# A graph layer with a sorted scatter: 48 directly summed edge columns in f32 against 72 in three exact bf16 addends

## The chip, the cores and the metric

One core of one Trainium2 chip runs the kernel. The metric is the device time of one execution in microseconds (us); smaller is better. Three runs of the kernel before give 2962.37 us as their median (2954.45 to 2979.23).

## The reference

There are N = 6250 nodes with 128 features and E = 206250 edges with 128 features each. An edge adds its features to the row of its source node. Then come a linear layer over node, sum and a global row, two softplus layers, a last linear layer, a residual and a normalization over the features:

```python
edge_aggr = jnp.zeros((n, HIDDEN), dtype=x.dtype).at[row].add(edge_features)
global_expand = jnp.repeat(global_feat, reps, axis=0)
combined = jnp.concatenate([x, edge_aggr, global_expand], axis=-1) @ W_c + b_c
h = jax.nn.softplus(combined @ W1 + b1)
h = jax.nn.softplus(h @ W2 + b2)
return h @ W3 + b3          # then: _layernorm(x + this)
```

All arrays are f32 except the edge's node numbers, which are int32 and in no order that the kernel may rely on. The sum over edges is what takes the time: everything behind it lies in the last 150 us of the profile.

## The kernel before, in words

The edges lie as 128 partitions by 1612 columns; a column is 128 edges, one per partition. The nodes lie in 25 blocks of 256 (`BL`), and `sums_t` holds the sums turned, features on the partitions and nodes along the free dimension (128 x 6400 f32). A column gets into `sums_t` in one of two ways.

**Gathered columns** (1564 of them). They are cut into the 11 groups of `GROUPS`, each a number of columns and the rows per partition of a chunk (`sub`). For each group:

- `node_codes` (line 209) and `positions` (line 247) work out on VectorE and TensorE where each edge goes when the group is sorted by block of nodes. Each block is padded to whole chunks of `sub` x 128 edges, so that 1564 columns become 2262 columns of chunks.
- `load_rows` (line 635) loads ten columns in one transfer on SP's queue, three pieces ahead (`LEAD`) in five buffers; `scatter_rows` (line 652) writes each column with an indirect DMA from GpSimd (line 658) to a place in DRAM, `place`. The place was filled with -1 beforehand (`fill_rows`, line 230).
- `reduce_steps` (line 396) takes a group back while the next one is scattered: `load` reads eight columns of chunks, `match` compares the edges' codes with the 256 nodes of a block (VectorE, line 428; in the last groups ScalarE too, lines 423 and 425, in shares by `TAIL`), `product` multiplies features by matches in f32 (line 442, a 128x256 product per column), and `add` adds the sum of a chunk to its block of `sums_t` (line 459). Three buffers of `part` in PSUM lie between product and addition.

**Directly summed columns** (`DIRECT` = 48, the first ones; `direct_steps`, line 550). They are not sorted. A set of 12 columns (`SET`) is loaded in one transfer (`load`, line 571), and is compared with all nodes, in 13 windows of 512 (`WIDE`; the last has 256). A job is two columns (`QUAD`) against one window: `compare` gives 1 where the edge's node is the window's node, as max(0, 1 - |node - number|), by two activations on 128x512 and one on 128x1024 on ScalarE (lines 582 and 584); `add` multiplies the columns' features by it in f32 (line 594) and gathers the six jobs of a set and window in one PSUM tile, `direct_sum`; `total` adds that to `sums_t` (line 602). `begin` works out on VectorE the node numbers and, in `less`, their distance from each window's first node. There are 4 x 13 x 6 = 312 jobs. The step of job i does the comparison of job i, the product of job i - 2, and a total that has come due, three steps behind its last product.

**The order.** On TensorE, VectorE, ScalarE and SP the instructions stand in the order in which the program gives them. GpSimd's scatters follow in their own queue. All loads and stores of SP go in one order (`put_dma`, line 148). The main loop runs over the groups and, in each, over its pieces of ten columns: it issues a piece's load, codes and scatter, and then a share of four lists, the positions of the next group (`prep`), the reduction of the group before (`sums`), the work on the nodes' own rows in groups 3 to 5 (`other`) and the fill of the next place (`filled`), each by `AHEAD`. Direct steps are dealt out by `left` (line 702): group g from 1 to 6 gets steps in proportion to its columns less a third of the chunk columns of group g - 1 (less 9 more in groups 3 to 5). That makes 43, 63, 58, 52, 52 and 50 steps in groups 1 to 6. Below, stage g is the time from the first scatter of group g to the first of group g + 1.

The last part, behind the groups, computes the layers on 13 tiles of up to 512 nodes.

## Time and profile before

| | |
|---|---|
| three runs, median (lowest to highest) | 2962.37 us (2954.45 to 2979.23) |
| the profiled execution, its time | 2979.23 us |
| its span, first to last instruction | 2977.4 us |
| mean granted TensorE clock | 0.823 |
| busy: TensorE, VectorE, ScalarE, GpSimd | 1948.8, 1326.4, 963.2, 1587.9 us |
| first and last scatter | 25.8 and 2826.8 us |
| first scatter of groups 1 to 8 | 81.3, 264.1, 643.4, 1075.6, 1500.1, 1931.9, 2346.5, 2571.8 us |
| direct products (line 594) | 1248 records from 104.5 to 2357.2 us |
| gathered products (line 442) | 4524 records |

An f32 product stands in the trace as two records, a bf16 product as one. PE is TensorE's matmuls, PEld its weight loads, DVE VectorE, ACT ScalarE, POOL GpSimd and SP the engine whose queue issues most transfers. Matmuls are pipelined, so the distance from start to start tells their price and their shown duration does not. A row of the groups gives the busy time, the mean duration, and the idle time of the engine just before, with what ended most of it; `remote` is a release that the profile can't name. A row of the windows gives the bounds and length of a stretch, the busy time and number of instructions of each engine, the granted TensorE clock as a share of full speed, the share of the DMA engines' time and GB/s.

### The profile page before, as it was taken

What the parts mean: (1) busy time and instruction counts of PE and PEld (TensorE: products, weight loads), DVE (VectorE), ACT (ScalarE), POOL (GpSimd) and SP (SyncE); (2) the same over time, 40 slices, a digit from 0 to 9 for tenths busy, and PEclk for the clock granted to TensorE, in tenths of its full rate; (3) what the DMA queues carried; (4) which work ended last, traced back from release to release, by engine and by line L of the source; (5) the groups of instructions that cost most, each with busy time, mean ns of one, the idle gap of its engine ahead of it and who ended that gap; (6) DMA issues with size and microseconds to landing.
All of it is one profiled execution on the core that took longest, in us unless ns stands there. A gap on an engine that the chain in (4) does not pass through costs nothing.

```text
span 2977.4 us, 21943 instructions
## 1 busy us (share of the span) xinstructions
PE 1948.8 (65%) x6470; PEld 1261.6 (42%) x6470; DVE 1326.4 (45%) x1961; ACT 963.2 (32%) x1313; POOL 1587.9 (53%) x1782
## 2 busy tenths in 40 slices
PE   2244586763876845887737768628777558747876
PEld 0022243431544532554424545415545446635663
DVE  5233353522453423554314644316454356525566
ACT  0223373423432313233204223205233100024596
POOL 5766435565355554655663465563655555554405
PEclk9867797776887967988868878869988778868898
DMA  9777445653464642555543445534445445545632
GB/s 294 210 209 231 116 127 161 186 148 93 136 171 138 184 127 92 149 157 153 143 129 95 140 119 147 146 91 119 135 137 154 142 123 178 179 120 144 177 86 87
DMA packets 418894, 437.21 MB, mean 147 GB/s; under 512 B 37807, under 2 KB 308774, under 8 KB 418774
## 3 DMA queue, kind: packets, MB, share of 16 engines
q1 hardware_dynamic: 368582, 332.43, 39.8%
q0 software_dynamic: 50048, 103.35, 10.5%
q8 instruction: 52, 0.85, 0.1%
q14 instruction: 68, 0.56, 0.1%
q10 hardware_dynamic: 144, 0.02, 0.0%
HBM read 262.62 MB, written 173.03 MB: 146 GB/s over the span
## 4 chain that ended last, share of the span: by engine, by line
PE 47%; another core or an unknown queue 24%; issue 14%; DVE 7%; ACT 7%; DVEq 0%; DMA 0%; ACTq 0%
PE part L442 29%; PE direct_sum L594 14%; ACT direct_hot L582 2%; ACT direct_hot L584 2%; DVE hot L428 2%; ACT hot L423 2%; DVE sums_t L459 1%; PE small L343 1%; DVE so_far L320 1%; PE small L277 0%; PE small L339 0%; PE small L340 0%; PE small L338 0%; ACT away L787 0%
## 5 line engine op out<-in xcount | busy, mean ns | idle before, releaser
L658 POOL DMA_INDIRECT place<-rows,pos x1564 | 1505.4, 963 | 1281.0 <-DMA rows<-in_edge_attr 598.2
L442 PE MATMUL part<-hot,chunks 128*128 128x256 f32 x4524 | 1183.1, 413 | 652.7 <-issue 340.6
L442 PEld LDWEIGHTS part<-hot,chunks 128*128 128x128 f32 x4524 | 926.5, 208 | 931.9 <-issue 458.0
L582 ACT ACTIVATE direct_hot<-iota_f,less 128x512 f32<-128x512 f32 (+1 forms) x624 | 404.2, 695 | 1595.9 <-remote 838.7
L594 PE MATMUL direct_sum<-direct_hot,direct_rows 128*128 128x512 f32 (+1 forms) x1248 | 633.7, 639 | 189.1 <-ACT direct_hot L584 108.7
L459 DVE TENSOR_TENSOR sums_t<-sums_t,part 128x256 f32 x808 | 339.0, 420 | 882.0 <-remote 568.4
L428 DVE SCALAR_TENSOR_TENSOR hot<-chunks,iota_ps 128x2048 f32<-128x2048 f32 (+1 forms) x251 | 570.6, 2274 | 0.0
L594 PEld LDWEIGHTS direct_sum<-direct_hot,direct_rows 128*128 128x128 f32 x1248 | 252.6, 208 | 446.8 <-issue 302.8
L584 ACT ACTIVATE direct_hot<-direct_hot,ones 128x1024 f32<-128x1024 f32 (+1 forms) x312 | 348.0, 1115 | 10.1
L423 ACT ACTIVATE hot<-iota_f,chunks 128x256 f32<-128x256 f32 x258 | 106.5, 494 | 381.2 <-PE part L442 299.6
L352 DVE TENSOR_TENSOR at<-small,ib 128x500 f32<-128x500 f32 (+3 forms) x80 | 52.9, 662 | 105.1 <-remote 71.0
L354 DVE TENSOR_REDUCE pos<-at 128x20 int32<-128x500 f32 (+3 forms) x80 | 87.0, 1088 | 2.7
L320 DVE TENSOR_TENSOR_SCAN so_far<-iota_ps,ib 128x1500 bf16<-128x1500 f32 (+7 forms) x30 | 85.9, 2862 | 0.0
L602 DVE TENSOR_TENSOR sums_t<-sums_t,direct_sum 128x512 f32<-128x512 f32 (+1 forms) x52 | 34.5, 663 | 111.1 <-PE direct_sum L594 64.5
L533 DVE COPY x_t<-small 128x512 f32<-128x512 f32 (+1 forms) x13 | 8.6, 659 | 150.1 <-remote 115.3
L541 DVE TENSOR_SCALAR z_x<-small,z_bias 128x512 f32<-128x512 f32 (+1 forms) x13 | 9.3, 718 | 136.1 <-remote 95.6
L425 ACT ACTIVATE hot<-hot,ones 128x2048 f32<-128x2048 f32 (+2 forms) x34 | 65.1, 1914 | 1.1
L864 POOL TENSOR_TENSOR x_sb<-x_sb,b_all 128x512 f32<-128x512 f32 (+1 forms) x13 | 15.3, 1213 | 81.7 <-DMA x_sb<-in_x 81.7
L293 DVE TENSOR_REDUCE size_f<-small 128x25 f32<-128x500 f32 (+1 forms) x11 | 7.4, 674 | 115.0 <-remote 69.5
L339 PE MATMUL small<-so_far,ones_h 128*128 128x500 bf16 (+3 forms) x80 | 33.4, 417 | 21.7 <-issue 17.0
L266 DVE TENSOR_TENSOR ib<-block,iota_ps 128x1500 bf16<-128x1500 bf16 (+7 forms) x30 | 44.4, 1503 | 0.0
L277 PE MATMUL small<-ib,ones_h 128*128 128x500 bf16 (+3 forms) x80 | 24.9, 422 | 28.6 <-DVE ib L266 16.5
(117 smaller groups left out, 531.7 us busy)
## 6 DMA issues: line engine op xcount, KB each, us to landing
chunks<-place SPq DMA_DIRECT2D x281, 516.0 KB
rows<-in_edge_attr SPq DMA_DIRECT2D x154, 640.0 KB
place<-fill SPq DMA_DIRECT2D x252, 258.0 KB
place<-rows,pos POOLq DMA_INDIRECT x1564
x_sb<-in_x SPq DMA_DIRECT2D x24, 256.0 KB
direct_rows<-in_edge_attr SPq DMA_DIRECT2D x4, 768.0 KB
out<-y SPq DMA_DIRECT2D x12, 256.0 KB
src_i<-in_src SPq DMA_DIRECT2D x1, 761.5 KB
```

What stands on the lines that cost most here:

```text
L320: nc.vector.tensor_tensor_scan(t, iota_ps[:, 1:2].to_broadcast([P, NB * n]), in_block[k][0], 0.0, op0=ALU.mult, op1=ALU.add)
L352: nc.vector.tensor_mul(at, got.pop((k, j0)), in_block[k][1][:, :, j0:j1])
L354: nc.vector.tensor_reduce(pos[:, a - c0 + j0:a - c0 + j1], at.rearrange("p b g -> p g b"), axis=mybir.AxisListType.X, op=ALU.add)
L423: nc.scalar.activation(hot[:, j], codes, AF.Abs, bias=chunks[i][:, j, D:W], scale=-1.0)
L425: nc.scalar.activation(hot[:, :m], hot[:, :m], AF.Relu, bias=ones[:, :1], scale=-1.0)
L428: nc.vector.scalar_tensor_tensor(hot[:, :m], chunks[i][:, :m, D:W].to_broadcast([P, m, BL]), code_of(g), iota_ps.unsqueeze(1).to_broadcast ...
L442: nc.tensor.matmul(part[:, s - q, :], t[:, s * sub + j, :D], hot[:, s * sub + j], start=(j == 0), stop=(j == sub - 1))
L459: nc.vector.tensor_add(here, here, part[:, s - q, :])
L582: nc.scalar.activation(hot[:, j, :n], iota_f[:, :n], AF.Abs, bias=less[:, w, c + q + j:c + q + j + 1], scale=-1.0)
L584: nc.scalar.activation(hot[:, :, :n], hot[:, :, :n], AF.Relu, bias=ones[:, :1], scale=-1.0)
L594: nc.tensor.matmul(sum_of[c, w][:, :n], rows_in[c][:, q + j, :], hot[:, j, :n], start=(q + j == 0), stop=(q + j == k - 1))
L658: s = nc.gpsimd.indirect_dma_start(out=dst, out_offset=bass.IndirectOffsetOnAxis(ap=at, axis=0), in_=rows[:r, j, :], in_offset=None)
```

## The change

- `DIRECT` goes from 48 to 72 (six sets, 468 jobs); group 6 goes from 226 to 202 columns, so that the gathered columns are 24 fewer (1540, in 2238 columns of chunks). The direct steps become 476, in groups 1 to 6 by the same rule 67, 98, 90, 81, 81 and 61.
- The comparisons' result, `direct_hot`, is bf16. ScalarE's instructions are the same three per job.
- Each column's features are written as a sum of three bf16 numbers. The upper half of an f32 is read as the first where it lies; `split`, new, works on VectorE: the rest behind the first, the rest behind the upper half of that rest into `direct_low`, and a copy of the upper half of the rest into the lower half of the f32's own place. A set of 12 columns takes 18 such instructions on 128x256, in twos of columns (`SPLIT`). The f32 product of a column (two records) becomes three bf16 products with weight loads of their own.
- `less` is worked out per set (128x156) in `split`, not once for all in `begin`. `split` for the next set stands at the last window but one of a set, five windows (30 jobs) behind the set's load.
- The first set's load stands in group 0's last piece, ahead of that piece's `load_rows`; before, it was the second step of group 1, behind `begin`. The first `split` follows `begin` there.

Totals still come three steps behind the last product, and the shares of ScalarE in the last groups (`TAIL`) are the same.

```diff
...
 LOAD_COLS = 10
 EPS = 1e-5
-GROUPS = ((40, 1), (120, 2), (200, 4), (240, 4), (240, 4), (240, 4), (226, 4), (130, 2), (72, 2),
+GROUPS = ((40, 1), (120, 2), (200, 4), (240, 4), (240, 4), (240, 4), (202, 4), (130, 2), (72, 2),
           (38, 1), (18, 1))
 SOONER = 6
...
 CHUNK_ROWS = 1024
 PLACES = 3
-DIRECT = 48
+DIRECT = 72
 SET = 12
 WIDE = 512
 QUAD = 2
+SPLIT = 2
 FILL = 4
 POS_COLS = 20
 PART_COLS = 60
...
         def direct_steps():
             steps = []
             if not ND:
                 return steps
             NW = -(-NB * BL // WIDE)
-            less = keep.tile([P, NW, ND], F32, name="less")
-            rows_in, hot_of, sum_of = {}, {}, {}
+            node_f = keep.tile([P, ND], F32, name="node_f")
+            first = keep.tile([P, NW], F32, name="first")
+            less_of = {}
+            rows_in, low_in, hot_of, sum_of = {}, {}, {}, {}
             def begin():
-                first = keep.tile([P, NW], F32, name="first")
                 nc.gpsimd.iota(first, pattern=[[WIDE, NW]], base=0, channel_multiplier=0,
                                allow_small_or_imprecise_dtypes=True)
-                part, node, _ = whole_nodes(0, ND)
-                nc.vector.tensor_copy(node, part)
-                nc.vector.tensor_tensor(
-                    less, node.unsqueeze(1).to_broadcast([P, NW, ND]),
-                    first.unsqueeze(2).to_broadcast([P, NW, ND]), op=ALU.subtract)
+                part, _, _ = whole_nodes(0, ND)
+                nc.vector.tensor_copy(node_f, part)
             def load(c):
                 n = min(SET, ND - c)
...
                 sync_dma(rows_in[c][:, :n],
                          edge_attr[:P * T, :].rearrange("(p t) d -> p t d", p=P)[:, c:c + n, :])
+            def halves(t):
+                return [t.bitcast(BF16).rearrange("p c (d h) -> p c d h", h=2)[:, :, :, h]
+                        for h in (0, 1)]
+            def split(c):
+                n = min(SET, ND - c)
+                less = less_of[c] = direct_p.tile([P, NW, SET], F32, name="less", bufs=2)
+                nc.vector.tensor_tensor(
+                    less[:, :, :n], node_f[:, c:c + n].unsqueeze(1).to_broadcast([P, NW, n]),
+                    first.unsqueeze(2).to_broadcast([P, NW, n]), op=ALU.subtract)
+                low_in[c] = direct_p.tile([P, SET, D], BF16, name="direct_low", bufs=2)
+                for a in range(0, min(SET, ND - c), SPLIT):
+                    b = min(a + SPLIT, SET, ND - c)
+                    rest = direct_p.tile([P, SPLIT, D], F32, name="direct_rest")[:, :b - a]
+                    x_c = rows_in[c][:, a:b]
+                    nc.vector.tensor_sub(rest, x_c, halves(x_c)[1])
+                    nc.vector.tensor_sub(low_in[c][:, a:b], rest, halves(rest)[1])
+                    nc.vector.tensor_copy(halves(x_c)[0], halves(rest)[1])
             def compare(c, w, q):
                 n = min(WIDE, NB * BL - w * WIDE)
-                hot = direct_p.tile([P, QUAD, WIDE], F32, name="direct_hot", bufs=3)
+                hot = direct_p.tile([P, QUAD, WIDE], BF16, name="direct_hot", bufs=3)
                 hot_of[c, w, q] = hot
                 for j in range(QUAD):
                     nc.scalar.activation(hot[:, j, :n], iota_f[:, :n], AF.Abs,
-                                         bias=less[:, w, c + q + j:c + q + j + 1], scale=-1.0)
+                                         bias=less_of[c][:, w, q + j:q + j + 1], scale=-1.0)
                 nc.scalar.activation(hot[:, :, :n], hot[:, :, :n], AF.Relu, bias=ones[:, :1],
                                      scale=-1.0)
...
                 hot = hot_of.pop((c, w, q))
                 if q == 0:
                     sum_of[c, w] = ps.tile([P, WIDE], F32, name="direct_sum", bufs=2)
-                for j in range(QUAD):
-                    nc.tensor.matmul(sum_of[c, w][:, :n], rows_in[c][:, q + j, :], hot[:, j, :n],
-                                     start=(q + j == 0), stop=(q + j == k - 1))
+                for j in range(q, q + QUAD):
+                    addends = halves(rows_in[c][:, j:j + 1]) + [low_in[c][:, j:j + 1]]
+                    for i, part in enumerate(addends):
+                        nc.tensor.matmul(sum_of[c, w][:, :n], part[:, 0], hot[:, j - q, :n],
+                                         start=(j == 0 and i == 0), stop=(j == k - 1 and i == 2))
                 if q + QUAD == k:
                     ready.append((c, w, n))
...
             jobs = [(c, w, q) for c in range(0, ND, SET) for w in range(NW)
                     for q in range(0, min(SET, ND - c), QUAD)]
-            steps += [begin, lambda: load(0)]
+            steps += [lambda: load(0), begin, lambda: split(0)]
             ready, behind = [], []
             for i in range(len(jobs) + 6):
...
                         c, w, q = jobs[i]
                         if (w, q) == (NW // 2, 0) and c + SET < ND:
                             load(c + SET)
+                        if (w, q) == (NW - 2, 0) and c + SET < ND:
+                            split(c + SET)
                         compare(*jobs[i])
                     if 1 < i < len(jobs) + 2:
                         add(*jobs[i - 2])
...
             for g in range(1, G - 4):
                 left[g] = max(0.0, groups[g][1] - groups[g][0]
                               - groups[g - 1][3] * groups[g - 1][2] / 3 - (9 if 3 <= g < 6 else 0))
+            direct_first = direct[:1]
+            direct = direct[1:]
             direct_at = 0.0
             i = 0
             assert G > 6
...
                 filled = fill_rows(g + 1)
                 done = [0, 0, 0, 0]
                 for q in mine:
+                    if g == 0 and q == mine[-1]:
+                        for step in direct_first:
+                            step()
                     load_rows(i + LEAD)
                     code_rows(i)
                     scatter_rows(i)
```

## The prediction

> **What bounds the kernel now.** I read the page first, then the windows by stage (a stage runs from the first scatter of one group of columns to the first of the next), then the timeline inside single stretches. The page:
>
> ```profile
> span 2977.4 us, 21943 instructions
> PE 1948.8 (65%) x6470; PEld 1261.6 (42%) x6470; DVE 1326.4 (45%) x1961; ACT 963.2 (32%) x1313; POOL 1587.9 (53%) x1782
> PE 47%; another core or an unknown queue 24%; issue 14%; DVE 7%; ACT 7%; DVEq 0%; DMA 0%; ACTq 0%
> L658 POOL DMA_INDIRECT place<-rows,pos x1564 | 1505.4, 963 | 1281.0 <-DMA rows<-in_edge_attr 598.2
> ```
>
> No engine is full. TensorE (PE) carries 47% of the chain that ended last, and 24% belongs to waits that the profile can't name. GpSimd's scatters wait 598 us for rows, which SP sends in one queue with loads that wait for TensorE. The unnamed waits lie in the long runs of scatters:
>
> ```profile
> 1527.14 0.98 POOL L658 DMA_INDIRECT place<-rows,pos  x1 [1.60 <-issue]
> 1528.43 0.96 POOL L658 DMA_INDIRECT place<-rows,pos  x1 [0.30 <-issue]
> ...
> 1563.78 1.33 ACT L582 ACTIVATE direct_hot<-iota_f,less 128x512 f32<-128x512 f32 x2 [46.92 <-remote]
> ...
> 1572.38 2.93 PE L442 MATMUL part<-hot,chunks 128*128 128x256 f32 x6 [41.09 <-DVE hot L428]
> ```
>
> The columns are start, duration, engine and line, operation, idle time before it. A scatter of one column issues every 1.27 us; while they run without a break, TensorE, and what waits for it, stands still for 41 to 47 us. Counted over the timeline from 81 to 2571 us: in the first 15 us of a run of scatters TensorE starts 3.1 to 3.4 matmul records per us, after 30 us fewer than 0.6, and it recovers some 5 us after the run ends. Then SP's queue moves, rows land, and the next run begins. So a stage is a part that goes with the scatters, plus the time that TensorE needs in between, and there TensorE is dense:
>
> ```profile
> 1191.11 1.88 PE L594 MATMUL direct_sum<-direct_hot,direct_rows 128*128 128x512 f32 x4
> 1192.82 0.80 PE L277 MATMUL small<-ib,ones_h 128*128 128x500 bf16 x3
> 1193.47 3.61 PE L442 MATMUL part<-hot,chunks 128*128 128x256 f32 x16
> 1196.92 1.88 PE L594 MATMUL direct_sum<-direct_hot,direct_rows 128*128 128x512 f32 x4
> ```
>
> Starts give prices at full clock. A direct job (two columns against 512 nodes in f32, four records) takes 1192.82 - 1191.11 = 1.71 us; three bf16 matmuls of 500 take 0.65 us, 0.217 each, weight loads hidden; 16 gathered records take 3.45 us, 0.216 each.
>
> ```profile
> 264.10:643.40 379.30, 244.06 (x704) 135.52 (x702) 152.07 (x218) 160.83 (x207) 196.13 (x219) 0.80 0.52 150
> 1931.90:2346.50 414.60, 284.99 (x971) 186.90 (x970) 192.04 (x249) 121.12 (x153) 222.23 (x250) 0.84 0.43 127
> 2346.50:2571.80 225.30, 147.42 (x597) 118.73 (x596) 116.97 (x140) 1.63 (x3) 127.43 (x142) 0.80 0.53 158
> ```
>
> These are stages 2, 6 and 7 (time, then PE, PEld, DVE, ACT, POOL busy, granted TensorE clock, DMA). Stage 7 has 130 scatters, 568 gathered records and next to no direct work: 568 x 0.216 / 0.80 = 153 us of TensorE, so 72 us are left, **0.555 us per scattered column**. In stage 6 (227 scatters, 689 gathered records, 51 direct jobs) 126 us for the columns and 689 x 0.216 / 0.84 = 177 us leave 112 us, **2.19 us per direct job**, against 1.71 / 0.84 = 2.04 from the spacing. Stage 2 (200, 358, 68 jobs) gives 2.53 against 2.14. So a direct job costs its TensorE time at the granted clock and a little more: TensorE outside its still stretches is the bound.
>
> **The change part by part.** The sum is against the profiled execution, 2979.2 us (span 2977.4). The median of the three runs is 16.8 us lower, 2962.4; I apply the sum to that.
>
> *Direct jobs.* Before: 48 / 2 x 13 = 312, after: 72 / 2 x 13 = 468. One window in 13 is half as wide, so 300 and 450 full ones. Each goes from four f32 records to six bf16 matmuls, three addends for each of two columns. 512 columns at 0.217 x 512 / 500 = 0.222 us are 1.33 us per job; by the spacing of the f32 records (1.71 / 8 passes of 512) it is 1.28. I take 1.30. At the run's mean granted clock, 0.82: 2.085 before, 1.585 after. 450 x 1.585 - 300 x 2.085 = 713 - 625.5 = **+88 us**. Bounds: at full clock after, 450 x 1.30 - 625.5 = -41; at the whole-stage price of 2.3, of which only TensorE's 0.5 falls away, 450 x 1.8 - 300 x 2.3 = +120. I take the middle, since the row nearest to a job is its own spacing.
>
> *Twenty-four columns fewer in group 6.* 24 scatters, three loads of rows, 24 padded columns of 2262: 24 x 0.555 = **-13 us**; 48 gathered records in stage 7, 48 x 0.216 / 0.82 = **-13 us**. Three matches and six additions fewer on VectorE lie beside them.
>
> *VectorE's splitting.* Per set of 12 columns: 18 operations on 128x256 and one `less` of 128x156.
>
> ```profile
> L203 DVE TENSOR_TENSOR node<-node,wrap 128x240 f32<-128x240 f32 x3 | 1.2, 409 | 0.1
> L567 DVE TENSOR_TENSOR less<-node,first 128x624 f32<-128x624 f32 x1 | 0.9, 868 | 0.1
> ```
>
> 18 x 0.42 + 0.25 = 7.8 us in one block, five times in mid-stream. Behind it on VectorE stand the next match (line 428, for which TensorE waits) and the additions that free `part` and `direct_sum`. If it always falls into a still stretch it costs nothing, if never, 39 us; 4 in 10 lie outside, **+16**. It reads rows whose load SP issues 30 jobs earlier (over 100 us in stage 2), so it shouldn't wait.
>
> *Further additions.* 26 of 0.68 us (52 rows of line 602 become 78), 18 us of VectorE over six stages at 45% busy: nothing; at worst 18.
>
> *The start.* The first load of direct rows moves from SP's 99.4 us to ahead of the rows load at 87.4 us; SP then carries 768 KB earlier. In exchange VectorE waits for that load and splits for 8 us before ScalarE can follow. Now the first direct product waits for that load until 104.5 us. It evens out: nothing; -10 to +15.
>
> *ScalarE.* The comparisons are as many per job, 156 jobs more. Here is what one takes:
>
> ```profile
> 739.17 1.32 ACT L582 ACTIVATE direct_hot<-iota_f,less 128x512 f32<-128x512 f32 x2
> 740.52 1.15 ACT L584 ACTIVATE direct_hot<-direct_hot,ones 128x1024 f32<-128x1024 f32 x1
> 741.58 1.32 ACT L582 ACTIVATE direct_hot<-iota_f,less 128x512 f32<-128x512 f32 x2
> ```
>
> 2.41 us from job to job, so 468 x 2.41 = 1128 us against 752, in a span of which ScalarE has 32% now. The trace has no activation with a bf16 result; I take the f32 price, as nothing in the rows goes by width. In stages 1 and 2 the planner puts 164 jobs where it put 107: 395 us of ScalarE in 562. Three buffers of `direct_hot` let it work ahead while TensorE stands still, so I take nothing, and up to +130 as the end (the rival below).
>
> The Trainium skill has a rule that speaks against hoping here (page "ScalarE: Activation LUTs", section "What ACT_TABLE_LOAD costs"): an activation goes at one element per cycle and lane for fp32 and bf16 alike. If instead bf16 halved the time per element, a job would take some 1.2 us and ScalarE's total would fall to about 560 us; by the rule it stays 1128. No run here shows it yet; the sum is the same by both, as it goes by TensorE, and only the ScalarE rival would vanish.
>
> Sum: 88 - 13 - 13 + 16 = **+78 us**: 3057 against the profiled execution, 2962 + 78 = **3040 us** against the median.
>
> **The rivals.**
>
> *Faster: the bf16 jobs run at full clock* (12%). If the denser stream keeps the clock granted and a job costs 1.30 us instead of 1.585, the jobs cost -41, with the columns -67 and no price for the splitting: 2895 us. It turns at a price per job of (625.5 + 26) / 450 = 1.45 us, a granted clock of 0.90. For it: the bf16 rows hide their weight loads. Against it: no stage between 81 and 2789 us is granted over 0.84, and the still stretches that let it fall remain.
>
> *Faster: the time goes by scattered columns alone* (8%). Stages 2 to 6 take 1.77 to 1.90 us per column, whatever they hold; 24 x 1.8 = -43: 2919 us. Against it: the planner gives each stage work in proportion to its columns, so this proves little, and stage 1 with less TensorE work takes 1.52.
>
> *Slower by more: ScalarE becomes the bound in stages 1 and 2* (14%). There a job then costs 2.41 us: 164 x 0.96 x 2.41 = 380, against 250 at 1.585: +130 more, 3170 us. For it: 4.9 jobs per ten columns in stage 2 are 11.8 us of ScalarE, and TensorE has about 10.7 us free of standing still. Against it: the buffers filled ahead.
>
> *Slower by more: VectorE's blocks all lie open* (6%): 39 + 18 in place of 16: 3081 us.
>
> *Nothing* (4%): the gains and losses cancel, 2962 us.
>
> **How the numbers follow.** My own case has 56%, about 2990 to 3085 us by the bounds of its terms. 8 in 10 lie between 2915 and 3130: the column rival is in, the full-clock rival's middle out, and the upper end of the ScalarE rival out. Within 1% (about 30 us, what a measurement of this kernel can tell from none) are "nothing", a little of my case and the nearer part of the clock rival: 0.16. Faster by more: 0.19, from the two rivals. Slower by more: 0.65.
>
> **What would show it.** In the page after: 2808 direct matmuls at 0.21 to 0.22 us from start to start at full clock (six in 1.3 us); line 442's records 48 fewer. Stage 6 and 7 shorter together by some 35 to 45 us, stages 2 to 5 longer by 15 to 35 each; scatters at 1.27 us in their runs as before. If ScalarE bounds, TensorE's waits for `direct_hot` grow by over 100 us in stages 1 and 2. If VectorE does, TensorE's waits for the match behind each split show 5 us or more. Wrong is the whole if the stages 2 to 5 don't lengthen, or if a job's price in them falls below 1.45 us; wrong too if TensorE no longer stands still in runs of scatters.

## The result and the profile after

The changed kernel takes 3108.05 us (median of four runs, 3090.03 to 3120.84), the kernel before in the same measurement 2958.41 us (four runs): a ratio of 1.0489, interval 1.0404 to 1.0574. It is slower, as forecast, by 150 us where 78 were forecast. The profiled execution took 3120.84 us (span 3119.1) against 2979.23, 142 us more; the working below goes by these two.

The page of the kernel after, against the four lines of the page of before that the prediction shows:

```profile
span 3119.1 us, 25411 instructions
PE 1996.4 (64%) x7869; PEld 1274.6 (41%) x7977; DVE 1368.0 (44%) x2089; ACT 1321.5 (42%) x1781; POOL 1566.4 (50%) x1756
PE 37%; another core or an unknown queue 27%; ACT 15%; issue 13%; DVE 7%; DVEq 0%; DMA 0%; ACTq 0%
L687 POOL DMA_INDIRECT place<-rows,pos x1540 | 1484.1, 964 | 1444.9 <-DMA rows<-in_edge_attr 685.0
```

ScalarE's busy time rises by 358 us and its share of the chain that ended last from 7% to 15%. TensorE's share of the chain falls from 47% to 37%, and the scatters wait 685 us for rows where they waited 598. (TensorE's 7869 records are 108 short of its 7977 weight loads; those matmuls are missing from the trace.)

Where the time lies by stages. The view of busy times in stretches, kernel after, stages 1 to 7 (columns: time, PE, PEld, DVE, ACT, POOL busy with counts, granted TensorE clock, DMA share, GB/s):

```profile
81.80:283.30 201.50, 85.56 (x299) 39.05 (x307) 56.49 (x92) 84.14 (x105) 118.31 (x132) 0.74 0.71 201
283.30:707.80 424.50, 256.67 (x1020) 135.79 (x1039) 168.09 (x252) 241.17 (x309) 196.21 (x220) 0.79 0.48 136
707.80:1161.80 454.00, 306.80 (x1250) 185.63 (x1270) 189.22 (x255) 233.60 (x303) 236.54 (x264) 0.82 0.48 138
1161.80:1623.80 462.00, 310.67 (x1229) 196.75 (x1249) 192.80 (x236) 193.24 (x246) 236.30 (x265) 0.80 0.42 125
1623.80:2068.80 445.00, 309.70 (x1217) 197.04 (x1237) 190.18 (x238) 191.87 (x244) 236.50 (x266) 0.82 0.44 127
2068.80:2479.70 410.90, 281.62 (x1124) 187.31 (x1144) 192.15 (x251) 151.29 (x189) 198.59 (x224) 0.83 0.41 121
2479.70:2712.30 232.60, 145.00 (x585) 114.52 (x584) 111.17 (x135) 4.78 (x9) 127.45 (x142) 0.77 0.49 147
```

| stages | length before | length after | change | the prediction's own prices for them |
|---|---|---|---|---|
| 1 and 2 | 562.1 | 626.0 | +64 | +28 |
| 3, 4 and 5 | 1288.5 | 1360.9 | +72 | +62 |
| 6 and 7 | 639.9 | 643.5 | +4 | -29 |
| 8 to 10 | 256.3 | 258.2 | +2 | 0 |

The last column spreads the price of jobs (2.085 us each before, 1.585 after, by ScalarE's jobs in the stage, one against the narrow window counted as half) and of columns over the stages; VectorE's 16 us come on top, anywhere. So two things went otherwise: stages 1 and 2 grew by 36 us more than TensorE's jobs were priced at, and stages 6 and 7, with 24 scatters and 48 gathered records fewer, didn't shrink, which is 33 us more than the prices say. Stages 3 to 5 are 10 us above them.

Stage 2 of the kernel after, the timeline in a stretch without scatters (start, duration, engine and line, operation, idle time before):

```profile
676.05 1.32 ACT L606 ACTIVATE direct_hot<-iota_f,less 128x512 bf16<-128x512 f32 x2
677.40 1.15 ACT L608 ACTIVATE direct_hot<-direct_hot,ones 128x1024 bf16<-128x1024 bf16 x1
678.45 1.32 ACT L606 ACTIVATE direct_hot<-iota_f,less 128x512 bf16<-128x512 f32 x2
679.80 1.15 ACT L608 ACTIVATE direct_hot<-direct_hot,ones 128x1024 bf16<-128x1024 bf16 x1
680.86 1.32 ACT L606 ACTIVATE direct_hot<-iota_f,less 128x512 bf16<-128x512 f32 x2
...
682.23 0.98 POOL L687 DMA_INDIRECT place<-rows,pos  x1 [25.11 <-issue]
```

ScalarE goes from job to job in 2.40 to 2.41 us without a pause, and GpSimd's next scatter comes after 25.11 us of idle time. And the chain of waits inside stage 2, shares by line, first the kernel before, then the kernel after:

```profile
by line: another core or an unknown queue 32.4%; PE direct_sum L594 18.7%; PE part L442 14.5%; issue 10.7%; ACT direct_hot L582 9.9%; ACT direct_hot L584 8.8%; PE small L277 0.8%; DVE so_far L320 0.8%; PE small L343 0.6%; DVE hot L428 0.5%; 
```

```profile
by line: another core or an unknown queue 40.5%; ACT direct_hot L606 22.7%; ACT direct_hot L608 20.8%; PE direct_sum L620 7.4%; issue 6.2%; PE part L444 5.4%; DVE hot L430 0.6%; DVE sums_t L461 0.6%; PE small L345 0.3%; PE small L341 0.2%; 
```

Of stage 2's 379 us the comparisons carried 18.7% (71 us), of its 424 us they carry 43.5% (185 us); direct products and gathered products together fell from 33.2% to 12.8%. So by the chain of waits the bound of stage 2 moved from TensorE to ScalarE. It is no wide margin: as counted further down, 262 us of the stage are free of the still stretches, ScalarE is busy for 216 of them, and TensorE has some 200 us of work in the stage at its full-clock prices.

The direct products themselves, kernel after, at a granted clock of 1.00 (timeline):

```profile
1484.17 0.38 PE L620 MATMUL direct_sum<-direct_hot,direct_rows 128*128 128x512 bf16 x1
1484.60 0.38 PE L620 MATMUL direct_sum<-direct_hot,direct_low 128*128 128x512 bf16 x1
1484.82 0.59 PE L620 MATMUL direct_sum<-direct_hot,direct_rows 128*128 128x512 bf16 x2
1485.25 0.38 PE L620 MATMUL direct_sum<-direct_hot,direct_low 128*128 128x512 bf16 x1
1485.46 0.59 PE L620 MATMUL direct_sum<-direct_hot,direct_rows 128*128 128x512 bf16 x2
```

From the job's start at 1484.17 to the next job's at 1485.46 are 1.29 us; 1.30 was taken. (One of the first job's six records is missing from the trace.)

### The profile page after: what moved, and what is told of

It reads as the page before. It is cut to its first block, busy times and chain, and to the rows that moved or that the text cites. A ratio compares the mean times of both kernels' runs of the same rounds, so it can differ in the third digit from the quotient of the medians.

```text
span 3119.1 us, 25411 instructions
## 1 busy us (share of the span) xinstructions
PE 1996.4 (64%) x7869; PEld 1274.6 (41%) x7977; DVE 1368.0 (44%) x2089; ACT 1321.5 (42%) x1781; POOL 1566.4 (50%) x1756
## 4 chain that ended last, share of the span: by engine, by line
PE 37%; another core or an unknown queue 27%; ACT 15%; issue 13%; DVE 7%; DVEq 0%; DMA 0%; ACTq 0%
PE part L444 23%; PE direct_sum L620 10%; ACT direct_hot L606 7%; ACT direct_hot L608 6%; DVE hot L430 2%; DVE sums_t L461 2%; ACT hot L425 1%; DVE so_far L322 1%; PE small L345 1%; PE small L341 0%; PE small L340 0%; PE small L342 0%; ACT away L821 0%; PE small L279 0%
## 5 line engine op out<-in xcount | busy, mean ns | idle before, releaser
L444 PE MATMUL part<-hot,chunks 128*128 128x256 f32 x4476 | 1143.9, 410 | 443.6 <-DVE hot L430 211.9
L606 ACT ACTIVATE direct_hot<-iota_f,less 128x512 bf16<-128x512 f32 (+1 forms) x936 | 604.6, 693 | 1374.1 <-remote 888.8
L620 PE MATMUL direct_sum<-direct_hot,direct_rows 128*128 128x512 bf16 (+1 forms) x1771 | 576.6, 403 | 427.3 <-ACT direct_hot L608 209.5
L430 DVE SCALAR_TENSOR_TENSOR hot<-chunks,iota_ps 128x2048 f32<-128x2048 f32 x248 | 563.9, 2275 | 0.0
L608 ACT ACTIVATE direct_hot<-direct_hot,ones 128x1024 bf16<-128x1024 bf16 (+1 forms) x468 | 521.9, 1115 | 15.2
L620 PEld LDWEIGHTS <-direct_rows 128*128 128x128 bf16 x1872 | 189.5, 103 | 689.0 <-issue 532.6
L620 PE MATMUL direct_sum<-direct_hot,direct_low 128*128 128x512 bf16 (+1 forms) x929 | 373.8, 402 | 58.6 <-issue 54.1
L620 PEld LDWEIGHTS <-direct_low 128*128 128x128 bf16 x936 | 96.6, 103 | 179.2 <-issue 93.8
L354 DVE TENSOR_TENSOR at<-small,ib 128x500 f32<-128x500 f32 (+2 forms) x79 | 52.2, 661 | 97.3 <-remote 68.2
L356 DVE TENSOR_REDUCE pos<-at 128x20 int32<-128x500 f32 (+2 forms) x79 | 85.5, 1083 | 2.8
```

Of the source, the lines that this page charges most:

```text
L354: nc.vector.tensor_mul(at, got.pop((k, j0)), in_block[k][1][:, :, j0:j1])
L356: nc.vector.tensor_reduce(pos[:, a - c0 + j0:a - c0 + j1], at.rearrange("p b g -> p g b"), axis=mybir.AxisListType.X, op=ALU.add)
L430: nc.vector.scalar_tensor_tensor(hot[:, :m], chunks[i][:, :m, D:W].to_broadcast([P, m, BL]), code_of(g), iota_ps.unsqueeze(1).to_broadcast ...
L444: nc.tensor.matmul(part[:, s - q, :], t[:, s * sub + j, :D], hot[:, s * sub + j], start=(j == 0), stop=(j == sub - 1))
L606: nc.scalar.activation(hot[:, j, :n], iota_f[:, :n], AF.Abs, bias=less_of[c][:, w, q + j:q + j + 1], scale=-1.0)
L608: nc.scalar.activation(hot[:, :, :n], hot[:, :, :n], AF.Relu, bias=ones[:, :1], scale=-1.0)
```

## The experiments

Twelve kernels, in four series. Three facts are needed to read them. First, a series' kernels ran on one chip, beside the kernel before, and the chips differ widely: on those of the second and fourth series the kernel before took 2912.67 and 2957.9 us, as in the first measurement, but on those of the first and third 2164.79 and 2161.41 us. Times are compared inside a series only. Second, I call "still" the time from 17 us after the start of a run of scatters longer than 19 us (scatters that start less than 2.5 us apart; the run ends 1.27 us behind its last start) to 6 us after its end, and "free" the rest of a stage; both are counted from the timeline. Third, "TensorE's work" is counted from its records in the stage at the full-clock prices of the prediction (1.71 us a job in f32, 1.30 in bf16, times 0.96 for the narrow window; 0.216 a gathered record).

**First series: parts undone, on the first quick chip.**

*The kernel after with 48 direct columns: only the three addends and the splitting.*

```diff
-GROUPS = ((40, 1), (120, 2), (200, 4), (240, 4), (240, 4), (240, 4), (202, 4), (130, 2), (72, 2),
+GROUPS = ((40, 1), (120, 2), (200, 4), (240, 4), (240, 4), (240, 4), (226, 4), (130, 2), (72, 2),
...
-DIRECT = 72
+DIRECT = 48
```

> The kernel after with 48 direct columns again (group 6 back at 226): the bf16 addends, bf16 matches and the splitting alone, against the kernel before at 2958 us. TensorE theory (a direct job costs its matmuls at the granted clock): 300 full jobs save 0.50 us each, three splits in mid-stream cost some 9: 2958 - 150 + 9 = about 2820. ScalarE theory (jobs cost ScalarE's 2.41 us where they stand close): there are as many comparisons as before, so the gain is small, 2900 to 2950. VectorE theory (the splits lie open and cost more than 8 us each): 2860 to 2900, with waits for the match behind each split.

Measured: 2167.29 us, ratio to before 1.0011 (1.0002 to 1.0021).

*72 columns, in f32 products without splitting.*

```diff
...
-                    nc.vector.tensor_sub(rest, x_c, halves(x_c)[1])
...
-                hot = direct_p.tile([P, QUAD, WIDE], BF16, name="direct_hot", bufs=3)
+                hot = direct_p.tile([P, QUAD, WIDE], F32, name="direct_hot", bufs=3)
...
-                    addends = halves(rows_in[c][:, j:j + 1]) + [low_in[c][:, j:j + 1]]
...
+                    nc.tensor.matmul(sum_of[c, w][:, :n], rows_in[c][:, j, :], hot[:, j - q, :n],
+                                     start=(j == 0), stop=(j == k - 1))
```

> The kernel after with f32 products and f32 matches (72 direct columns, the distances still worked out per set, no splitting of the features): the 24 further columns alone. TensorE theory: 150 more full jobs at 2.085 us, 26 us less for the gathered columns: 2958 + 313 - 26 = about 3245. ScalarE theory: the comparisons are those of the kernel after, so the time is near the kernel after, 3110 to 3150.

Measured: 2177.76 us, ratio 1.0058 (1.0042 to 1.0075).

*The kernel after without the second activation of a comparison.*

```diff
-                nc.scalar.activation(hot[:, :, :n], hot[:, :, :n], AF.Relu, bias=ones[:, :1],
-                                     scale=-1.0)
```

> The kernel after without the second activation of a comparison; the products then multiply by the distance instead of by the match, so the sums are others. ScalarE's job falls from 2.41 to 1.26 us, TensorE's and VectorE's work stays. ScalarE theory: the part over the TensorE sum goes away, 3108 - 70 to - 130 = 2980 to 3040, nearly all of it in stages 1 and 2. TensorE theory: within 15 us of 3108. VectorE theory: the same.

Measured: 2137.77 us, ratio 0.988 (0.9864 to 0.9897).

*The kernel after without the splitting, three products of the same upper half.*

```diff
-                low_in[c] = direct_p.tile([P, SET, D], BF16, name="direct_low", bufs=2)
-                for a in range(0, min(SET, ND - c), SPLIT):
...
-                    addends = halves(rows_in[c][:, j:j + 1]) + [low_in[c][:, j:j + 1]]
+                    addends = halves(rows_in[c][:, j:j + 1])[1:] * 3
```

> The kernel after without the splitting's 18 instructions per set; each column's three products all take the upper half of its features, so the sums are rounded. The number of matmuls and activations stays. VectorE theory: 3108 - 39 = 3070 or less. My sum: - 16, about 3090. ScalarE and TensorE theories: 3095 to 3108.

Measured: 2135.08 us, ratio 0.986 (0.9843 to 0.9876).

On this chip TensorE doesn't stand still (a granted clock of 0.95 to 1.00 in the stages shown below), so these four say nothing of where the 150 us went; they show what bounds the kernels there. The three addends with their splitting cost 2.5 us in all at 48 columns. The scatters' row of the 48-column kernel, from the groups by line:

```profile
L687 POOL DMA_INDIRECT place<-rows,pos x1564 | 1508.0, 964 | 482.1 <-issue 411.2 <-POOL rows L679 18.3 <-DMA place<-rows,pos 17.4
```

The scatters wait for rows no longer (598 us in the first profile of before, 685 in that of after): nearly all idle time ahead of them is the 0.30 us of issue between neighbours. Stage 2 shows it best. The view of stretches, stages 2 and 6, first of the kernel without the splitting, then of the one in f32:

```profile
239.70:494.70 255.00, 221.07 (x1023) 129.35 (x1021) 140.59 (x195) 241.69 (x317) 196.12 (x219) 0.99 0.77 219
1412.30:1669.70 257.40, 231.69 (x1048) 167.07 (x1048) 177.41 (x234) 119.94 (x153) 198.62 (x223) 0.95 0.65 188
```

```profile
240.00:494.90 254.90, 248.24 (x781) 139.55 (x780) 140.36 (x195) 218.81 (x287) 196.23 (x220) 1.00 0.79 219
1422.00:1711.40 289.40, 275.28 (x1000) 181.84 (x1000) 189.83 (x249) 150.42 (x187) 198.63 (x223) 0.99 0.63 171
```

200 scatters take 255 us, 1.27 us each, in one run without a break, and TensorE works through it at a clock of 0.99. So here GpSimd is the bound, and 24 columns fewer are worth 24 x 1.27 = 30 us: the kernels without the splitting and without the second activation gained 30 and 27 us. Only f32 at 72 columns leaves that bound: TensorE is 95% busy in stage 6 (275.28 of 289.40), and the kernel is 42.7 us slower than with three bf16 products and no splitting. That is a measured reason for the addends: on this chip 72 columns in f32 overfill TensorE.

**Second series: the number of direct columns, on a chip that is like the first measurement's.** The kernel before and the kernel after unchanged, the kernel after with 96 columns (the first diff), the kernel before with 24 (the second).

```diff
-GROUPS = ((40, 1), (120, 2), (200, 4), (240, 4), (240, 4), (240, 4), (202, 4), (130, 2), (72, 2),
+GROUPS = ((40, 1), (120, 2), (200, 4), (240, 4), (240, 4), (240, 4), (178, 4), (130, 2), (72, 2),
...
-DIRECT = 72
+DIRECT = 96
```

```diff
-GROUPS = ((40, 1), (120, 2), (200, 4), (240, 4), (240, 4), (240, 4), (226, 4), (130, 2), (72, 2),
+GROUPS = ((40, 1), (120, 2), (212, 4), (240, 4), (240, 4), (240, 4), (238, 4), (130, 2), (72, 2),
...
-DIRECT = 48
+DIRECT = 24
```

> The kernel before, unchanged, once more with a trace. The experiments so far ran where the kernel before takes 2165 us and where scatters issue every 1.27 us without a break; the first two profiles, where it takes 2958, have TensorE standing still in long runs of scatters. Theory of the place (the stillness belongs to the chip or its condition, not to the kernel): 2165 us again and one unbroken run of scatters in the trace, TensorE at 3 and more records per us throughout; or about 2960 with the still stretches, if it runs where the first two did. Theory of the profiler (the stillness comes from tracing): the trace shows still stretches while the untraced times are lower by hundreds of us.

Measured: 2916.52 us, beside 2912.67 for the other runs of the same kernel. The standing still is there again, and the times without a profile lie within 3% of the profiled one, so it isn't made by the profiling.

> The kernel after, unchanged, beside the kernel before. Scatter theory (where TensorE doesn't stand still, GpSimd's scatters are the bound): 24 scatters fewer at 1.27 us, 30 us less than before, about 2135 where before takes 2165. TensorE theory (the sum of the prediction holds anywhere): slower by 78 us or more. Where before takes about 2960, about 3108 as on record.

Measured: 3074.96 us, ratio 1.0546 (1.0427 to 1.0666): the first result again, though the runs of the kernel before spread from 2881.62 to 2962.29 us here. By stages it is the first result too: stages 1 and 2 grew by 88 us (545.6 to 633.6), 3 to 5 by 68 (1257.2 to 1325.4), 6 and 7 not at all (627.3 to 627.5).

> The kernel after with 96 direct columns and group 6 at 178: another 24 columns moved. Scatter theory: 30 us less again, about 2105 where before takes 2165, unless TensorE or ScalarE (2.41 us x 624 jobs = 1504 us) fill up in stages 1 to 6, in which case the scatters show breaks and it is slower than the kernel after. Where TensorE stands still: about 3108 + 150 = 3260.

Measured: 3183.85 us, ratio 1.0954 (1.087 to 1.1039). Against the kernel after, stages 1 to 5 take 164 us more, but stages 6 and 7 are 50 us shorter (577.4), with as many scatters fewer (24) as had gained nothing from 48 to 72 columns.

> The kernel before with 24 direct columns (groups 2 and 6 take 12 more each). Scatter theory: 24 scatters more at 1.27 us, 2195 where before takes 2165. Where TensorE stands still: 150 full jobs fewer at 2.1 to 2.3 us and 24 columns more at 1.3, 2958 - 315 to 345 + 31 = 2640 to 2680.

Measured: 2887.27 us, ratio 0.9948 (0.9895 to 1.0002). A clear miss: 156 direct jobs in f32, priced at 2.085 us each, were taken away, and of some 290 us only 25 were gained, which can't be told from none.

Two stages of the four kernels, counted as said above, in profiled executions of 2911, 2928, 3075 and 3188 us (ScalarE's busy time is that of the view of stretches):

| stage, kernel | columns | length | free | ScalarE busy | TensorE's work | still | runs of scatters, mean length |
|---|---|---|---|---|---|---|---|
| 2, f32, 24 | 212 | 346 | 146 | 83 | 125 | 200 | 6, 53 us |
| 2, before, 48 | 200 | 365 | 203 | 153 | 181 | 162 | 8, 32 us |
| 2, after, 72 | 200 | 438 | 249 | 242 | 204 | 189 | 6, 41 us |
| 2, bf16, 96 | 200 | 475 | 345 | 325 | 245 | 130 | 10, 24 us |
| 3, f32, 24 | 240 | 417 | 196 | 74 | 184 | 221 | 8, 35 us |
| 3, before, 48 | 240 | 418 | 216 | 150 | 225 | 203 | 10, 27 us |
| 3, after, 72 | 240 | 436 | 262 | 230 | 247 | 174 | 13, 21 us |
| 3, bf16, 96 | 240 | 495 | 352 | 324 | 301 | 144 | 15, 19 us |

The free time goes with the larger of the two engines' work (0.96 to 1.17 times it): TensorE's with 24 and 48 columns, ScalarE's with 72 and 96 in stage 2 and with 96 in stage 3. TensorE's work alone doesn't account for it: with 72 and 96 columns the free time of stage 2 is 1.22 and 1.41 times that. And the still time isn't a price per column. In stage 3 it falls as the free time grows (221, 203, 174, 144 us), and the same 240 scatters come in more and shorter runs; in stage 2 it doesn't from 48 to 72 columns (162, 189). (Where a run is taken to end moves single figures: with gaps counted from a scatter's end, these two would be 191 and 203.) So the kernel with 24 columns won nothing in stage 3: 20 us less of free time, 18 us more standing still. The two windows, kernel before and then 24 columns:

```profile
629.70:1048.10 418.40, 290.34 (x907) 172.64 (x906) 167.39 (x202) 150.26 (x189) 235.20 (x264) 0.82 0.52 149
```

```profile
606.30:1023.10 416.80, 255.71 (x821) 167.57 (x821) 172.08 (x209) 73.75 (x96) 234.84 (x263) 0.74 0.53 151
```

86 TensorE records and half of ScalarE's time are gone, the length is the same, and the granted clock is lower, 0.74.

That ScalarE fills stage 2 is plainest with 96 columns, in a stretch of 175 us with only 54 instructions on GpSimd, and in the chain of waits of that stage:

```profile
390.00:565.00 175.00, 132.95 (x589) 68.69 (x588) 76.55 (x129) 162.67 (x212) 48.61 (x54) 0.99 0.40 111
```

```profile
by line: ACT direct_hot L606 25.8%; ACT direct_hot L608 23.0%; another core or an unknown queue 19.9%; PE direct_sum L620 11.3%; PE part L444 9.3%; issue 8.2%; DVE direct_rest L596 0.5%; DVE direct_low L597 0.5%; DVE hot L430 0.5%; DVE sums
```

ScalarE is busy for 93% of the stretch, TensorE for 76% at a clock of 0.99, and the comparisons carry 48.8% of the chain of stage 2 (in the same series 37.5% with 72 columns and 12.0% with 48; 43.5% and 18.7% in the first profiles).

**Third series: breaks in the runs of scatters.** If standing still comes from the unbroken runs, breaks that cost GpSimd time must still gain. Six idle writes of 128x240 after each ten scatters, asked for in that place by an order laid on GpSimd's scatters and writes, in the kernel before; beside it, again, the kernel after without the second activation.

```diff
+    idle = const.tile([P, 240], F32, name="idle")
...
+            if k == LOAD_COLS:
+                for _ in range(6):
+                    m = nc.gpsimd.memset(idle, 0.0)
...
```

> Once more the kernel after without the second activation of a comparison (the products multiply by the distance, so the sums are others), for a place where TensorE stands still in long runs of scatters. Known there: before 2913, after 3075 (ratio 1.055). ScalarE theory: the part of the loss that ScalarE makes in stages 1 and 2, 60 to 100 us by the chains of those stages (ScalarE 255 us of stages 1 and 2 in the kernel after, 77 in the kernel before), goes away: ratio to before 1.02 to 1.035, stages 1 and 2 together 540 to 580 us long. TensorE theory: ratio 1.05 to 1.06. Where TensorE doesn't stand still: 2138 beside 2165 as in the first run of it.

Measured: 2133.62 us, ratio 0.9873 (0.9857 to 0.989).

> The kernel before with six memsets of an unused tile on GpSimd behind each piece of ten scatters, some 2.5 us in which it issues none. Theory of the long runs (TensorE stands still once scatters have been issued for some 17 us without a break, and gaps of 2 to 3 us, as between 2433 and 2475 us of the first profile, keep it going): a piece takes 15.2 us at most instead of 17.5 to 18, TensorE at 3 records per us throughout, 2600 to 2700 us where before takes 2913. Theory of the work (the still stretches are only TensorE waiting for something else): the breaks add up, 2913 + 0 to 390 us. Where TensorE doesn't stand still: 2165 + 154 x 2.5 = 2550 us, all of it loss.

Measured: 2441.35 us, ratio 1.1295 (1.1276 to 1.1314).

This series fell to another quick chip (before: 2161.41 us). There the 924 idle writes, 281 us busy on GpSimd, cost 280 us: where GpSimd bounds and TensorE doesn't stand still, the whole price is paid. The kernel without the second activation gains 28 us there, as it gained 27 in the first series.

**Fourth series: the breaks again, with the kernel after.**

> The kernel after, unchanged, once more; known: 1.049 and 1.055 times the kernel before where TensorE stands still in long runs of scatters, not yet measured where it doesn't. Scatter theory: where before takes 2161 to 2165 us, 24 scatters fewer at 1.27 us, 2130 to 2137 us, ratio 0.985 to 0.988, one unbroken run of scatters. TensorE theory (the sum of the prediction holds anywhere): ratio 1.02 or more. Where TensorE stands still: 1.045 to 1.06.

Measured: 3088.21 us beside 2957.9 for before, ratio 1.0488 (1.0388 to 1.0588): a third time the same result.

> The kernel before with 2.5 us without scatters behind each piece of ten, once more. Where TensorE doesn't stand still it was 2441 us beside 2161. Where it does: theory of the long runs 2450 to 2650 us beside 2913, with 3 TensorE records per us throughout; theory of the work 2913 or more.

Measured: 2531.39 us, ratio to before 0.8575 (0.8523 to 0.8628). On this chip a kernel with 281 us more work on GpSimd is 427 us faster, and it beats both kernels. Its timeline at a break, and its stages 2 and 5 (of 200 and 240 columns) in the view of stretches:

```profile
1207.57 0.95 POOL L660 DMA_INDIRECT place<-rows,pos  x1 [0.30 <-issue]
1208.51 2.10 POOL L671 MEMSET idle<- 128x240 f32 x6
1210.56 0.20 POOL L652 COPY rows<-src_i 128x10 f32<-128x10 f32 x1
1211.06 0.99 POOL L660 DMA_INDIRECT place<-rows,pos  x1 [0.30 <-issue]
```

```profile
259.50:563.00 303.50, 247.68 (x713) 133.11 (x712) 148.07 (x212) 174.84 (x224) 229.24 (x335) 0.89 0.64 181
1270.70:1626.20 355.50, 281.43 (x966) 186.20 (x966) 183.41 (x216) 122.73 (x156) 277.10 (x410) 0.87 0.50 154
```

Against the first profile of before, stage 2 takes 1.52 us per column instead of 1.90, stage 5 1.48 instead of 1.80. The page shows the unnamed wait gone from 24% to 8% of the chain:

```profile
span 2529.5 us, 22804 instructions
PE 43%; issue 23%; POOL 12%; another core or an unknown queue 8%; DVE 6%; ACT 5%; DMA 2%; DVEq 0%; SPq 0%; ACTq 0%; POOLq 0%
```

But the idle writes don't all stand where they were asked for. In the trace 112 groups of six stand together, a break of 2.5 us or more; 221 writes stand singly between two scatters, mostly around the start of a group of columns, and there the pause between scatters is only some 0.5 us instead of 0.30:

```profile
271.86 0.32 POOL L671 MEMSET idle<- 128x240 f32 x1
272.35 0.96 POOL L660 DMA_INDIRECT place<-rows,pos  x1 [0.16 <-issue]
```

This settles whether the break counts or the slower pace. Two stretches of this run, the first with single writes, the second with breaks, and then the stretch with single writes again, at the same place of the same kernel on the quick chip of the third series:

```profile
290.00:365.00 75.00, 38.44 (x60) 14.52 (x58) 8.34 (x5) 20.76 (x26) 62.33 (x93) 0.66 0.29 90
1000.00:1260.00 260.00, 220.79 (x780) 147.89 (x780) 150.27 (x173) 103.28 (x127) 202.26 (x301) 0.92 0.55 167
```

```profile
289.70:364.70 75.00, 69.15 (x217) 40.76 (x217) 49.39 (x63) 40.35 (x51) 62.60 (x93) 0.93 0.80 226
```

The pace is nearly one: 54 scatters in 75 us and 174 in 260, 0.72 and 0.67 per us. But with single writes TensorE starts 0.8 records per us, with breaks 3.0, and on the quick chip it starts 2.9 in the place where it starts 0.8 here. So long runs without a break of some 2.5 us are what costs the time on these chips; the three records per us that were expected throughout hold only where the breaks stand. What in the chip ties TensorE to the runs is not shown by any run.

## Why the prediction was right, and where it was not

The sign and the range were right: 3108 us lies between 2915 and 3130. The size was not (+150 against +78): 3108 lies above the 2990 to 3085 of the prediction's own case, and the jobs' term was too high where others were too low, so part of the nearness is luck. Its sign for stages 6 and 7, 35 to 45 us shorter, failed (+4). The terms of the sum one by one:

*Direct jobs, +88 us.* The full-clock price was right (1.29 us measured, 1.30 taken). Failed was the step "At the run's mean granted clock, 0.82". From stage 2 to the end of stage 6 the clock averages 0.92 in the free time of the kernel before and 0.94 in that of the kernel after, 0.68 and 0.59 in the still time; the mean of 0.82 mixes the two, and jobs are done mostly in the free time. At those clocks the term is 450 x 1.30 / 0.94 - 300 x 1.71 / 0.924 = +67. It is no price by which to add and take away jobs either, as the 24 columns showed (25 us of some 290): in stage 3 there, the 20 us of free time that were saved came back as 18 us of still time.

*Twenty-four columns, -13, and 48 gathered records, -13.* Failed: "72 us are left, 0.555 us per scattered column" read a price per column out of one stage. What scatters cost TensorE goes with how long their runs are, not with their number alone. In stage 7 the 130 scatters came in 6 runs of 29.7 us on average instead of 7 of 25.5, the still time grew from 82 to 96 us, and the stage lengthened by 7 us with fewer gathered records to do. In stage 6 the still time did fall, from 167 to 140 us, but the free time rose from 247 to 272, although TensorE's work there fell (232 to 223 us at full clock); what filled it is not shown. Stages 6 and 7 together changed by +4 where -29 came from these terms and the jobs. Nor is a column worth nothing: the next 24 fewer, in the kernel with 96 direct columns, shortened these stages by 50 us.

*VectorE's splitting, +16.* The blocks were sized rightly, 7.0 to 7.1 us against 7.8, but they hold up little. Groups by line of the kernel after, shapes apart:

```profile
L597 DVE TENSOR_TENSOR direct_low<-direct_rest 128x256 bf16<-128x256 f32 x36 | 15.4, 427 | 2.2 <-DVE direct_rest L596 1.1
L596 DVE TENSOR_TENSOR direct_rest<-direct_rows 128x256 f32<-128x256 f32 x36 | 15.3, 424 | 7.1 <-DVE direct_rows L599 2.9 <-remote 1.8 <-DMA direct_rows<-in_edge_attr 1.5
L599 DVE COPY direct_rows<-direct_rest 128x256 bf16<-128x256 bf16 x36 | 11.1, 307 | 0.0
```

The five blocks in mid-stream begin at 437.6, 754.1, 1068.4, 1494.8 and 1929.8 us. TensorE starts 16, 5, 27, 29 and 32 records during them, against 26, 1, 45, 45 and 40 in the 10 us before; per us that is 2.3, 0.7, 3.8, 4.1 and 4.5 against 2.6, 0.1, 4.5, 4.5 and 4.0. It slows by 15% at most, 1 us of a block: some 5 us in all at most, not 16. Removing the splitting was measured only on the quick chip, so the price on this kind stays an estimate from these counts.

*Totals, and the start, at nothing.* Both right as far as the trace shows: the first stretch is 55.8 us long instead of 55.5, and the totals' additions (78 of 0.67 us) are not among the ten largest parts of the chain of stage 2 shown above.

*ScalarE, at nothing.* This is the largest miss. The duration was right: a bf16 result takes ScalarE 693 and 1115 ns where f32 took 695 and 1115, and a job 2.41 us still, so the rule of the Trainium skill ("ScalarE: Activation LUTs", section "What ACT_TABLE_LOAD costs") agrees with this trace. Failed was the step "Three buffers of `direct_hot` let it work ahead while TensorE stands still, so I take nothing": three jobs ahead are 7 us of its work in front of 103 jobs that stage 2 asks of it, 241 us busy, of which only 25 fall into the 162 us of standing still and 216 into the 262 free ones. The rival was right about the place. Its price, +130, was too high: stages 1 and 2 grew 36 us beyond TensorE's price. In stage 2 the free time grew by 60 us (202 to 262), and 15 us of that came back from standing still (177 to 162), with shorter runs (30 us on average instead of 36); in the second series' pair the still time grew instead, so this return is not steady. The sign by which the prediction wanted to know it, waits of TensorE for `direct_hot`, grew in stages 1 and 2 from 59 to 117 us, not by over 100: the profile books much of that wait under other names. The chain of waits shows it better.

Where that leaves the 142 us between the profiles: at the clocks of the free time the jobs' +67 lie as +22 in stages 1 and 2, +49 in 3 to 5 and -4 in 6 and 7. The measured changes are 42, 24 and 7 us above that. The 42 go with ScalarE, as argued here; of the 24 at most 5 are the splitting, and the rest is not attributed.

*That TensorE's idle time comes with the runs of scatters* held in all three measurements of the two kernels, and the breaks confirm it by acting on GpSimd's queue alone. The prediction took it as given that this belongs to the kernel; two chips show that it does not always.

What stays open. Why two chips show none of the standing still. What the change does there: the kernel after itself wasn't run on one, but its two lightened forms, with the same scatters, were 27 and 30 us faster than before, so there the sign may well be the other. And the kernels with 48 columns in bf16 and without the second activation were not measured on a chip where TensorE stands still, so that taking ScalarE's load away would give the time of stages 1 and 2 back is argued from the table above, not shown.

## What to carry to other kernels

Split a stage into the time in which an engine is held up and the time in which it runs, and read the granted clock of each apart; a mean over both (0.82 here, from 0.94 and 0.59) prices nothing. Work that is made cheaper on one engine and more in number is paid on whichever engine is fullest in the stage where it lands: in stage 2 ScalarE's comparisons carried 43.5% of the chain and the direct products 7.4%, so a cheaper job on TensorE could help little there. And before trading work against a cost per item, change the number of items alone once: the price per scattered column, read from one stage, didn't hold where it was used. 24 scatters fewer left stages 6 and 7 as long as they were, the next 24 took 50 us off them, and breaks between the same scatters were worth 427 us.

## What was not expected of the hardware

- The same kernel before takes 2161 to 2165 us on two chips and 2913 to 2962 us on others. On the quick ones a run of scatters goes on unbroken and TensorE works through it (the kernel without the splitting, stage 2: 255.0 us at a clock of 0.99); on the others TensorE slows some 17 us into a run (in the first profile of before 3.1 records per us from 10 to 15 us into a run, 1.0 from 20 to 25, under 0.6 after 30).
- While it stands still, single TensorE instructions often start 0.7 or 1.4 us apart, and VectorE too starts late behind a matmul. The timeline of the kernel before, 53 to 67 us into a run:

```profile
670.88 0.38 PE L442 MATMUL part<-hot,chunks 128*128 128x256 f32 x1 [1.65 <-issue]
...
672.27 0.19 PEld L442 LDWEIGHTS part<-hot,chunks 128*128 128x128 f32 x1 [2.61 <-issue]
...
673.68 0.38 PE L442 MATMUL part<-hot,chunks 128*128 128x256 f32 x1 [2.42 <-issue]
...
683.49 0.88 DVE L459 TENSOR_TENSOR sums_t<-sums_t,part 128x256 f32 x2 [30.09 <-remote]
...
684.42 2.07 PE L442 MATMUL part<-hot,chunks 128*128 128x256 f32 x4 [10.36 <-issue]
```

  Product, weight load and product start 1.39 and 1.41 us apart. The last product that VectorE's addition needs ends at 674.06, and the addition begins at 683.49; outside such a stretch, at 1197.12, one follows 0.04 us behind the end of its product.
- On such a chip ten scatters and a break of about 2.5 us keep TensorE going at 3.0 records per us; single pauses of some 0.5 us between scatters don't (0.8 per us). The kernel with both takes 2531 us.
- Three exact bf16 products of 512 columns take 0.65 us at full clock where the f32 product takes 0.86 (jobs of two columns: 1.29 and 1.71 us).
